# Two attention layers on one core: each engine keeps the order of emission in place of list scheduling

## The chip, the cores and the metric

The kernel runs on one core of a Trainium2 chip. The metric is the device time of one launch in microseconds; lower is better. Before the change it was 3159.26 us, the median of 3 runs (3157.74 to 3161.56).

A core has engines that run side by side, each through its own queue of instructions: TensorE (PE, with PEld for its weight loads), VectorE (DVE), ScalarE (ACT), GpSimd (POOL) and SyncE (SP, which here only issues DMAs). An engine waits for another through semaphores. The order of instructions inside each engine's queue is fixed when the program is built, and that order is what the change touches.

## What is computed

The input has 4 images of 64 x 64 tokens with 256 channels. Two layers of self-attention follow each other, cut here to their core:

```python
# layer 0: 32 query/key channels, 256 value channels
q = x @ Wq + bq; k = x @ Wk + bk; v = x @ Wv + bv
x = gamma * (softmax(q @ k.T) @ v) + x
# layer 1: 32 query/key channels, 128 value channels, output projection
f = x @ Wf + bf; g = x @ Wg + bg; v = x @ Wh + bh
x = x + (softmax(g @ f.T) @ v) @ Wo + bo
```

Each image attends over its own 4096 tokens; the softmax is taken without subtracting a maximum, and a general path (launched only if a flag says that the values are too large) stands behind the fast one.

## The kernel before

`fast_path` walks through 4 images, 2 layers each. A layer is cut into blocks of queries `j` (16 blocks of 256 queries in layer 0, 8 blocks of 512 in layer 1) and a block into steps `i` over the keys (8 steps of 512 keys in layer 0, 16 steps of 256 keys in layer 1). Every step handles a 128 x 1024 tile of scores:

- PE writes the scores `st` (line 532) into PSUM.
- ACT takes the exponential into `p` (544) and, where the step is "split", a slightly scaled one, rounded to the faster matmul format, into `high` (542). All steps of layer 0 and 6 of the 16 of a block in layer 1 are split.
- DVE makes from them `low` (555) and then `d` (560), the parts that restore the lost digits. In layer 1 DVE also adds `p` up (`p_sum`, 571 and 573); for 5 of the 16 steps DMAs issued by POOL add it into `p_sum_moved` instead (548, 550).
- PE multiplies the parts with the values: in layer 0 three products for each of two halves of the queries, 24 matmuls in all (582); in layer 1 either six matmuls of the parts or two of the whole `p` (600).

Some buffers are scarce: one tile `d` in layer 0, two tiles (tag `t`) that `high`, and in split steps of layer 1 `p` too, share, one `st` in PSUM (every other step of layer 1 uses the tile `pair`, which holds accumulators in layer 0), one set of accumulators (`acc0`, `acc1`, `pair`), two side tiles in PSUM, and one `p_sum_moved`.

At the end of a block ("turn" below) ACT and DVE copy the accumulators out: lines 615 and 616 in layer 0, 651 and 657 in layer 1, where 659 and 660 also close the sum of `p`. Then come small units of work that the plan spreads over the steps of the next block: in layer 0 the division and the residual (625, 626, 628, and an addition on POOL, 639); in layer 1 four outputs `pso` (667 and 668 on PE, 670 on DVE, 673 on ACT).

The next layer is prepared in units for 256 tokens, three pieces each: the transpose piece (392 on DVE, 405 `xh` on ACT, 406 `xl` on DVE), the query/key piece (422 on PE, 439 ACT, 440 DVE, 441 ACT, 442 DVE, then DMAs), and the value piece (464 on PE, 480 and 481 on ACT, and for split tiles 482 and 483 on DVE). The plan puts one unit into each block `j >= 2` of layer 0 (steps 0, 4 and 5) and about two into each block of layer 1 in the first three images. The first 6 units stand before the first step of all, 10 more in its first block.

The order in which the kernel emits all this is written out by hand. For each step it is

```python
s.cut_both()                 # DVE: d of this step
after.cut_low()              # DVE: low of the next step
s.add_up(p_sum)              # DVE, layer 1
if l == 1:
    if s.last: o = take_first_two(b, j, acc)      # ACT 651
    later.scores()           # PE 532, ACT 542 and 544, two steps ahead
    run(todo)                # the units of this step
    ...                      # PE: h, l or the whole p; d of the step before
else:
    ...                      # PE: h (and l)
    later.scores()
    run(todo)
    ...                      # PE: d (and l)
if s.last: ends = end_first(b, j, acc) if l == 0 else end_second(b, j, acc, p_sum, o)
```

In the kernel before, this order is only the input of the compiler's list scheduler, which places the instructions of each engine by its own estimate of when their operands are ready. In the profiled program it put, for instance, the copy `o` of a finished accumulator (615) ahead of two exponentials that were emitted earlier.

Of the kernel before, what the change touches and what calls it, by code (L numbers as in the profile page):

```python
# [824 lines left out]
def tile_two_attention_layers(tc: tile.TileContext, *args):  # L825
    nc = tc.nc
    with tc.tile_pool(name="flag", bufs=1) as pool:
        off = pool.tile([1, 1], I32, name="off")
        fast_path(tc, *args, off)
        flag = nc.values_load(off[0:1, 0:1], min_val=0, max_val=4 * P, skip_runtime_bounds_check_because="a count")  # L830
        with tc.If(flag > 0):
            general_path(tc, *args)
# [40 lines left out]
```

## Time and profile before

| | |
|---|---|
| median of the runs | 3159.26 us (3157.74 to 3161.56) |
| profiled execution: span, first to last instruction | 3154.1 us |
| median less span (what lies around the instructions; the profiled execution has no separate time) | 5.2 us |
| PE busy | 3116.3 us, 99% |
| DVE busy | 2689.1 us, 85% |
| ACT busy | 2140.1 us, 68% |
| POOL busy | 900.7 us, 29% |
| granted TensorE clock | 0.998 of full |

The profile shows one execution. Busy time is the time in which an engine had an instruction running; a line of the groups gives the number of instructions, the mean duration in ns, and the idle time just before them with what ended it. The timeline gives the start in us, the duration, the engine, the source line, the operation and its tiles; `x4` means four in a row. The windows view gives the busy time of each engine in a stretch.

### The profile page before, as it was taken

How to read it: one execution, taken by the hardware profiler on the slowest of the kernel's cores; microseconds unless marked ns; L12 is line 12 of the kernel's file. 1: busy time of each engine (PE TensorE's matmuls, PEld its weight loads, DVE VectorE, ACT ScalarE, POOL GpSimd, SP SyncE). 2: the span in 40 equal slices, each digit the busy share in tenths (PEclk: the TensorE clock that was granted, in tenths of full speed). 3: DMA queues.
4: the chain of work that ended last, by engine and by line, in shares of the span. 5: the costliest groups of instructions: out<-in, count | busy, mean ns of one | idle time of the engine just before them, and what ended most of it. 6: DMA issues, size and time to landing. Idle time of an engine off the chain costs nothing.

```text
span 3154.1 us, 54090 instructions
## 1 busy us (share of the span) xinstructions
PE 3116.3 (99%) x19908; PEld 2672.0 (85%) x19908; DVE 2689.1 (85%) x3237; ACT 2140.1 (68%) x2835; POOL 900.7 (29%) x1108
## 2 busy tenths in 40 slices
PE   8999999999999999999999999999999999999997
PEld 7999998666799999866679999976668999996664
DVE  7888888888888888888888888898888888888876
ACT  7666666777666666777766666677776666666674
POOL 5232224222422222422242222232223222233221
PEclk9999999999999999999999999999999999999999
DMA  4121114555512121555541112255554111125454
GB/s 119 43 53 47 48 48 104 107 108 105 104 44 51 41 53 47 113 101 112 107 93 47 49 45 51 51 116 107 105 113 81 48 46 47 49 65 105 97 95 73
DMA packets 391392, 239.49 MB, mean 76 GB/s; under 512 B 266672, under 2 KB 355248, under 8 KB 391120
## 3 DMA queue, kind: packets, MB, share of 16 engines
q0 software_dynamic: 68160, 134.86, 22.0%
q1 hardware_dynamic: 322048, 100.76, 13.4%
q8 instruction: 161, 2.64, 0.4%
q14 instruction: 111, 0.91, 0.1%
q10 hardware_dynamic: 912, 0.33, 0.1%
HBM read 82.58 MB, written 67.11 MB: 47 GB/s over the span
## 4 chain that ended last, share of the span: by engine, by line
PE 91%; DVE 3%; DMA 2%; issue 2%; ACT 1%; POOL 0%; SPq 0%; DVEq 0%; ACTq 0%; POOLq 0%
PE acc L600 24%; PE acc L582 23%; PE acc_pair L582 23%; PE st L532 14%; PE psv L464 4%; PE psqk L422 2%; PE pso L667 2%; DVE d L560 1%; DVE low L555 1%; ACT p L544 1%; DVE p_sum L573 1%; DMA p_sum_moved<-p 0%; DMA squares<-in_x 0%; PE pso L668 0%; DMA squares<-x_dram 0%
## 5 line engine op out<-in xcount | busy, mean ns | idle before, releaser
L542 ACT ACTIVATE high<-st,down 128x1024 fp32r<-128x1024 f32 x704 | 786.5, 1117 | 703.2 <-PE st L532 362.8
L544 ACT ACTIVATE p<-st 128x1024 f32<-128x1024 f32 x1024 | 1042.5, 1021 | 166.3 <-PE st L532 143.8
L560 DVE SCALAR_TENSOR_TENSOR d<-low,high 128x1024 fp32r<-128x1024 f32 x704 | 871.0, 1237 | 227.0 <-PE acc_pair L582 223.7
L555 DVE TENSOR_TENSOR low<-p,high 128x1024 fp32r<-128x1024 f32 x704 | 936.6, 1330 | 142.6 <-ACT p L544 141.6
L532 PE MATMUL st<-q,k 128*128 128x256 f32 (+1 forms) x3072 | 706.3, 338 | 2.5 <-DMA k<-qk_parts 1.4
L600 PE MATMUL acc<-p,v 128*128 128x512 f32 x1280 | 611.0, 597 | 0.0
L532 PEld LDWEIGHTS st<-q,k 128*128 128x128 f32 x3072 | 470.0, 189 | 103.3 <-issue 40.6
L639 POOL TENSOR_TENSOR x_res<-x,bo 128x256 f32<-128x256 f32 x128 | 212.5, 1660 | 879.3 <-DVE x L628 879.2
L600 PEld LDWEIGHTS acc<-p,v 128*128 128x128 f32 x1280 | 233.1, 189 | 161.8 <-issue 143.4
L573 DVE TENSOR_TENSOR p_sum<-p_sum,p 128x1024 f32<-128x1024 f32 x288 | 352.6, 1224 | 9.4 <-ACT p L544 5.8
L582 PE MATMUL acc<-v0h,high 128*128 128x258 f32 x2048 | 341.6, 284 | 1.2 <-ACT high L542 1.2
L582 PE MATMUL acc<-v0d,d 128*128 128x258 f32 x2048 | 339.2, 287 | 2.6 <-DVE d L560 2.2
L582 PE MATMUL acc<-v0l,low 128*128 128x256 f32 (+1 forms) x2048 | 329.3, 283 | 0.6 <-DVE low L555 0.5
L582 PE MATMUL acc_pair<-v0h,high 128*128 128x258 f32 x2048 | 329.8, 283 | 0.0
L582 PE MATMUL acc_pair<-v0l,low 128*128 128x256 f32 (+1 forms) x2048 | 328.8, 282 | 0.0
L582 PE MATMUL acc_pair<-v0d,d 128*128 128x258 f32 x2048 | 328.5, 282 | 0.0
L582 PEld LDWEIGHTS acc<-v0h,high 128*128 128x128 f32 x2048 | 286.0, 189 | 3.1 <-issue 1.4
L582 PEld LDWEIGHTS acc<-v0d,d 128*128 128x128 f32 x2048 | 281.5, 190 | 5.6 <-DVE d L560 4.9
L582 PEld LDWEIGHTS acc<-v0l,low 128*128 128x128 f32 x2048 | 282.2, 190 | 1.8 <-DVE low L555 1.3
L582 PEld LDWEIGHTS acc_pair<-v0h,high 128*128 128x128 f32 x2048 | 282.1, 189 | 0.0
L582 PEld LDWEIGHTS acc_pair<-v0l,low 128*128 128x128 f32 x2048 | 281.1, 189 | 0.0
L582 PEld LDWEIGHTS acc_pair<-v0d,d 128*128 128x128 f32 x2048 | 281.0, 189 | 0.0
(108 smaller groups left out, 3332.5 us busy)
## 6 DMA issues: line engine op xcount, KB each, us to landing
p_sum_moved<-p POOLq DMA_DIRECT2D x160, 512.0 KB, 4.7
x_res<-in_x SPq DMA_DIRECT2D x128, 128.0 KB, 2.1
qk_dram<-qk_parts SPq DMA_DIRECT2D x128, 128.0 KB, 1.9
x_dram<-x SPq DMA_DIRECT2D x128, 128.0 KB, 1.7
out<-x_res SPq DMA_DIRECT2D x128, 128.0 KB, 1.7
squares<-x_dram SPq DMA_DIRECT2D x512, 32.0 KB, 1.9
out<-y POOLq DMA_DIRECT2D x128, 128.0 KB, 3.2
q<-qk_dram POOLq DMA_DIRECT2D x252, 64.0 KB, 2.2
```

The lines of the kernel that those rows point to most:

```text
L422: nc.tensor.matmul(ps, wqk[l][:, c, :], x_parts[key][n][:, c, :], start=(c == n == 0), stop=(c == NCC - 1 and n == 1),)
L464: nc.tensor.matmul(ps[:, t, :], xT[key][:, c, t * P : (t + 1) * P], wv[l][:, c, :], start=(c == 0), stop=(c == NCC - 1),)
L532: nc.tensor.matmul(st[:, g, :], k_t[b, l, kt // NT][:, kt % NT * P : (kt % NT + 1) * P], q_t[b, l, j * n // QB][:, q0 : q0 + n], start=Tru ...
L542: nc.scalar.activation(self.high, s_flat, AF.Exp, bias=down)
L544: nc.scalar.activation(self.p, s_flat, AF.Exp)
L555: nc.vector.tensor_sub(self.low, self.p, self.high.bitcast(F32))
L560: nc.vector.scalar_tensor_tensor(self.d, self.low.bitcast(F32), -UP, self.high.bitcast(F32), ALU.mult, ALU.add)
L573: nc.vector.tensor_add(p_sum, p_sum, self.p)
L582: nc.tensor.matmul(acc[2 * s + which][:, :width], p[:, g * QB0 + s * P : g * QB0 + (s + 1) * P], v0[self.i][v][:, g, :width], start=self.f ...
L600: nc.tensor.matmul(acc[which], v_part[:, g, :], p[:, g * QB : (g + 1) * QB], start=first and g == 0, stop=last and g == G[1] - 1,)
L639: nc.gpsimd.tensor_add(x_old[s], x_new[s], bo_sb)
L667: nc.tensor.matmul(ps[:, :C], part, wo_sb, start=True, stop=True)
```

## The change

One `with` block is put around the call of `fast_path`. Inside it the list scheduler does not reorder: each engine's queue holds its instructions, and SP and POOL their DMA issues, in the order of emission. Tiles, instructions, buffers and dependencies stay as they are.

```diff
     with tc.tile_pool(name="flag", bufs=1) as pool:
         off = pool.tile([1, 1], I32, name="off")
-        fast_path(tc, *args, off)
+        with tc.manual_schedule():
+            fast_path(tc, *args, off)
         flag = nc.values_load(off[0:1, 0:1], min_val=0, max_val=4 * P, skip_runtime_bounds_check_because="a count")
```

The built programs differ as follows, engine by engine. PE has 20701 instructions in both, and 16677 of them stand at the same place. In layer 0 PE's order differs mainly around the turns, where the scheduler had pulled matmuls of the next step ahead. ACT and DVE differ around the turns and around every unit. SP and POOL change by a few places.

## The prediction

> **What bounds the kernel now.** I read the busy times and the chain that ended last, then the windows by layer, then the timeline of a turn in each layer.
>
> ```profile
> PE 3116.3 (99%) x19908; PEld 2672.0 (85%) x19908; DVE 2689.1 (85%) x3237; ACT 2140.1 (68%) x2835; POOL 900.7 (29%) x1108
> ...
> PE 91%; DVE 3%; DMA 2%; issue 2%; ACT 1%; POOL 0%; SPq 0%; DVEq 0%; ACTq 0%; POOLq 0%
> ```
>
> PE is never short of work: 38 us of its 3154 are idle, 16 of them in the first 100 us by the windows view. So a better order has little to win, while every wait that a new order puts in front of PE counts in full.
>
> ```profile
> 100.00:520.00 420.00, 419.81 (x3499) 418.85 (x3499) 364.76 (x426) 276.66 (x352) 118.33 (x120) 1.00 0.21 52
> 524.00:857.00 333.00, 332.22 (x1286) 224.31 (x1285) 291.45 (x353) 240.54 (x335) 94.69 (x138) 1.00 0.58 110
> 2851.00:3133.00 282.00, 281.74 (x989) 180.00 (x989) 227.79 (x244) 193.19 (x228) 73.80 (x97) 1.00 0.51 98
> ```
>
> These are layer 0 of an image, layer 1 with units of the next image in it, and layer 1 of the last image without them (columns: PE, PEld, DVE, ACT, POOL busy, clock, DMA). In the first two DVE is busy 87% (364.76 of 420, 291.45 of 333): it has little time to stand in a queue.
>
> The turn of layer 0 from block 5 to 6, as scheduled:
>
> ```profile
> 264.60 1.02 ACT L544 ACTIVATE p<-st 128x1024 f32<-128x1024 f32 x1
> 265.51 0.62 ACT L405 CAST xh<-xT 128x512 fp32r<-128x512 f32 x1
> 265.65 1.23 DVE L555 TENSOR_TENSOR low<-p,high 128x1024 fp32r<-128x1024 f32 x1
> 265.74 0.68 PE L532 MATMUL st<-q,k 128*128 128x256 f32 x4
> 266.01 0.40 ACT L615 ACTIVATE o<-acc 128x258 f32<-128x258 f32 x1
> ...
> 266.50 1.12 ACT L542 ACTIVATE high<-st,down 128x1024 fp32r<-128x1024 f32 x1
> ...
> 267.51 1.02 ACT L544 ACTIVATE p<-st 128x1024 f32<-128x1024 f32 x1
> 267.70 0.64 PE L582 MATMUL acc<-v0h,high 128*128 128x258 f32 x4
> 267.94 1.22 DVE L560 SCALAR_TENSOR_TENSOR d<-low,high 128x1024 fp32r<-128x1024 f32 x1
> ```
>
> Two things to see: ACT copies the accumulator at 266.01, before the two exponentials, so that PE can overwrite it at 267.70 without a gap; and `xh` (transpose piece) sits in a hole of ACT. Four matmuls of this kind follow the next four at 0.48 us (267.70 to 268.18), so a plain step of 28 costs 3.35 us.
>
> **The change, part by part.** It removes and adds no work. I walk through the emitted order with the durations of these rows and ask when PE must wait. Between engines I take 0.05 to 0.1 us, and from the start of scores to the exponential 0.76 (265.74 to 266.50).
>
> *Turn of layer 0.* In emission order ACT does `high` and `p` first: 266.5 + 1.12 + 1.02 gives 268.63; `o` ends at 269.03. PE, ready at 267.58, waits 1.5 us for the accumulator. DVE adds the two `o` (0.42 each, to 269.95) before `d` (to 271.2), which PE needs at 271.0: 0.2 more. PE ends the step at 272.7; before, the same matmuls were done at 270.94. **1.75 us, 64 turns: 112.**
>
> *Transpose piece (step 0).* DVE transposes (0.70), then waits for `xh`, which stands behind the two exponentials of the step: `xh` ends at 274.1, `xl` 274.8, the queued `d` 276.05. PE wants it at 275.07. **1.0 us, 14 blocks per image, 56: 56.**
>
> *Query/key piece (step 4).* The chain copy 0.37, add 0.47, cast 0.41, subtract 0.42 goes four times between ACT and DVE, begins behind `p`, and now stands whole before `d` on DVE: `d` is ready about 0.75 us after PE asks, even with the value matmuls (0.95 us) as cover. **56 x 0.75: 42.** *Value piece (step 5):* for the 6 of 14 tiles that are split, two DVE operations wait for ACT and delay `d` by 1.65 us. **24 x 1.65: 40.** The other 8 cost nothing: the cover is 1.5 us of slack on ACT; gone, they would cost up to 0.8 each.
>
> *POOL beside DVE.* After a residual, POOL's addition slows `low`:
>
> ```profile
> 246.66 1.80 POOL L639 TENSOR_TENSOR x_res<-x,bo 128x256 f32<-128x256 f32 x1 [1.56 <-DVE x L628]
> ...
> 247.78 1.76 DVE L555 TENSOR_TENSOR low<-p,high 128x1024 fp32r<-128x1024 f32 x1
> ```
>
> 1.76 against 1.23 us: 0.53, twice per block, hidden today by about 0.9 us of slack; the walk leaves 0.2. I take 0.3 per block, **20** (0 to 64). [...] The row shows 0.53, and the sum goes by the row.
>
> Layer 0: **270** (low end 112, the turns alone; high 340).
>
> *Layer 1.* Its turn from block 2 to 3 in the trace:
>
> ```profile
> 642.64 1.22 DVE L659 TENSOR_TENSOR p_sum<-p_sum,p_sum_moved 128x1024 f32<-128x1024 f32 x1
> ...
> 644.44 0.55 POOL L548 DMA_DIRECT2D p_sum_moved<-p  x1 [6.92 <-ACT qk L439]
> ...
> 644.91 0.68 DVE L660 TENSOR_TENSOR sums<-p_sum 128x512 f32<-128x512 f32 x1
> ...
> 645.74 0.30 PE L668 MATMUL pso<-ones,sums 128*128 128x1 f32 x2
> ...
> 648.28 1.02 ACT L544 ACTIVATE p<-st 128x1024 f32<-128x1024 f32 x1 [0.51 <-DMA p_sum_moved<-p]
> ```
>
> Here the scheduler let PE run the queries/keys and a whole step before 668, and ACT an exponential of a later step before the one at 648.28 (which needs the buffer that the DMA of 644.44 reads, 3.84 us). In emission order both stand in line. Counting from the scores of step 1 of the new block: DVE does `low` (1.49), `p_sum` (2.7), transpose and, after `xh`, `xl` (4.8), the two `o` (5.7), 659 (6.9), 660 (7.6); PE's first `pso` then starts at 7.6 in place of 4.5: 3.1 us. The DMA starts after 659, so `p` of step 3 ends at 11.9, and behind it in ACT's queue stand `y`, which frees a side tile, and the query/key copy; PE waits for both before `pso` 1 and the value matmuls, then for `high` of step 5, which waits for `d` of step 3. At step 7 of this block PE is 6 us late, and two further units cost 2.8 at steps 11 to 15 (`p` of step 13 waits for `p_sum`, that waited for `xl` and the value piece). Block 3: 8.9 us. The same walk of block 5, with units at other steps: 7.5. Mean **8.2, 24 blocks: 197.** Without units `pso` waits 1.0 and smaller waits 0.5: **1.5 x 8: 12.** Layer 1: **209** (low 90 if half of the waits overlap; high 300).
>
> *Start.* Six units run before the first scores, which come at about 38 us in place of 22.3; the interleaved rest was slow before as well, so I take **10** (0 to 25).
>
> Sum 270 + 209 + 10 = 489: 3154.1 + 489 + 5.2 = **3648; I say 3650.**
>
> SP and POOL: 8 loads `squares` take 0.5 us each to issue and follow the query/key piece, whose store is now up to 2 us later; the next transpose comes 4 or 5 steps later (13 us), so nothing.
>
> *The clock.* The granted clock is 1.00 in all three windows, and the waits PE does have there are under 1 us. [...] The gaps of the walk stay at 1 to 3 us, and the sum has nothing for them.
>
> **The rivals.**
>
> *The waits overlap (0.17).* An engine freed by one stall of PE catches up, so that only the turns count: 112 + 24 x 3.1 + 8 x 1.0 + 10 = 204, thus 3363. For it: DVE has 13% spare. Against it: in the walk the waits lie 2 or more steps apart, and PE's delay does not shorten DVE's queue.
>
> *Faster (0.04).* The scheduler breaks groups: in the built program 21 of the 320 groups of whole-`p` matmuls in layer 1 are broken in two. After such a group the next takes 0.4 us more than otherwise (619.09 to 619.95 against 0.46), so 21 x 0.4 = 8 us come back, and PE's 38 idle us could shrink by a third: 3139. It decides only if all the queues' waits stay below PE's slack of about 0.9 us per step; at the turn of layer 0 `o` alone stands 2.1 us later.
>
> *It does nothing (0.02).* 16677 of PE's 20701 places are the same; if ACT's and DVE's order did not matter, 3159 within 6 us. DVE's order differs at every unit, which speaks against it.
>
> *Worse than walked (0.07).* DVE, 87% busy, becomes the bound in layer 1 with every wait on ACT in its queue, and PE's gaps grow beyond 3 us: 12 us per block, 24 x 3.8 = 91 more, and layer 0 at its high end, 70: 3810.
>
> **The numbers.** Forecast 3650 at 0.70. Its own low end is 112 + 90 + 0 = 202 (the first rival's place), its high end 340 + 300 + 25 = 665, 3824. Ends do not fall together, so I take 3420 to 3820, which leaves out most of the first rival and the small cases. About 0.2% (6 us) is what a measurement can tell from no change: faster 0.04, same 0.02, slower 0.94.
>
> **What would show it.** Right: PE's busy share falls to 84 to 88%; the period of a layer 0 block grows from 28.2 us to about 31.7, and to 33.3 where the value tile is split; a block of layer 1 grows by 7 to 10 us in the first three images and by 1 to 2 in the last; idle before 582 is put down to `o` of line 615 and to `d`, and before 668 to `sums`. Wrong: blocks of layer 0 at 30 us (only the turn counts), or PE idle that is put down to DMAs, or a clock below 1.00.

## The result, and the profile after

The changed kernel takes 3642.19 us (median of 4 runs, 3639.95 to 3644.05) against 3158.95 us for the kernel before (4 runs, 3157.74 to 3161.56): the ratio is 1.1534, with a 95% interval of 1.152 to 1.1548. The profiled execution took 3644.05 us with a span of 3642.3 us, 488.2 us more than the span before.

First the busy times and the chain that ended last:

```profile
PE 3274.0 (90%) x19908; PEld 2723.9 (75%) x19908; DVE 2722.6 (75%) x3237; ACT 2149.1 (59%) x2835; POOL 868.7 (24%) x1108
...
PE 46%; DVE 20%; ACT 19%; issue 8%; DMA 5%; POOL 1%; ACTq 0%; SPq 0%; DVEq 0%; POOLq 0%
```

No engine has more instructions than before, and none is full any more. PE holds 46% of the chain that ended last, DVE and ACT together 39%. Before, 91% of it lay on PE.

The windows of layer 0, of layer 1 with pieces of the next image, and of layer 1 of the last image (PE, PEld, DVE, ACT, POOL busy, then the clock and the DMA share):

```profile
140.00:580.00 440.00, 403.98 (x3266) 394.25 (x3265) 342.63 (x394) 258.73 (x329) 96.31 (x92) 1.00 0.17 43
612.00:945.00 333.00, 298.10 (x1046) 189.30 (x1046) 248.56 (x299) 206.06 (x287) 68.32 (x95) 0.97 0.48 92
3345.00:3610.00 265.00, 254.30 (x870) 158.45 (x868) 202.26 (x212) 172.54 (x197) 68.24 (x95) 0.99 0.49 92
```

PE is idle 36 us of 440, 35 of 333 and 11 of 265, and in layer 1 the clock is no longer 1.00.

The waits of PE by what ended them (us in total, times, longest):

```profile
PE acc L582 <- DVE d L560: 100.7, 136, 2.3
PE acc L582 <- ACT o L615: 59.6, 60, 1.0
PE pso L668 <- DVE sums L660: 35.1, 29, 1.5
PE st L532 <- DMA q<-qk_dram: 30.2, 14, 4.7
...
PE psqk L422 <- ACT y L673: 17.0, 8, 3.5
...
PE st L532 <- DMA k<-qk_dram: 11.2, 4, 3.0
```

The first three and the wait for `y` are ones that the prediction named. The two DMA waits it had not.

The turn of layer 0 from block 5 to 6, with the transpose piece behind it:

```profile
287.88 1.12 ACT L542 ACTIVATE high<-st,down 128x1024 fp32r<-128x1024 f32 x1 [1.14 <-PE st L532]
...
288.89 1.02 ACT L544 ACTIVATE p<-st 128x1024 f32<-128x1024 f32 x1
289.80 0.39 ACT L615 ACTIVATE o<-acc 128x258 f32<-128x258 f32 x1
...
290.24 0.75 PE L582 MATMUL acc<-v0h,high 128*128 128x258 f32 x4 [1.00 <-ACT o L615]
290.56 0.42 DVE L616 TENSOR_TENSOR o<-o,acc_pair 128x258 f32<-128x258 f32 x1
...
290.89 1.22 DVE L560 SCALAR_TENSOR_TENSOR d<-low,high 128x1024 fp32r<-128x1024 f32 x1
...
293.53 1.01 ACT L544 ACTIVATE p<-st 128x1024 f32<-128x1024 f32 x1
...
294.43 0.62 ACT L405 CAST xh<-xT 128x512 fp32r<-128x512 f32 x1
...
295.08 0.69 DVE L406 TENSOR_TENSOR xl<-xT,xh 128x512 fp32r<-128x512 f32 x1 [1.22 <-ACT xh L405]
...
295.69 1.22 DVE L560 SCALAR_TENSOR_TENSOR d<-low,high 128x1024 fp32r<-128x1024 f32 x1
...
296.96 0.75 PE L582 MATMUL acc<-v0d,d 128*128 128x258 f32 x4 [0.72 <-DVE d L560]
```

The copy `o` now stands directly behind `high` and `p`, and PE waits 1.00 us for it. In the next step `xh` stands behind `p` on ACT, so `xl` waits 1.22 us at the head of DVE's queue with `d` behind it, and PE waits 0.72 us for that `d`.

The turn of layer 1 from block 2 to 3 in the first image, the one that the prediction walks through:

```profile
758.90 0.70 PE L667 MATMUL pso<-wo,o 128*128 128x256 f32 x2 [0.97 <-DVE o L657]
759.09 1.22 DVE L659 TENSOR_TENSOR p_sum<-p_sum,p_sum_moved 128x1024 f32<-128x1024 f32 x1
760.35 0.69 DVE L660 TENSOR_TENSOR sums<-p_sum 128x512 f32<-128x512 f32 x1
760.89 0.56 POOL L548 DMA_DIRECT2D p_sum_moved<-p  x1 [17.19 <-DVE p_sum L659]
760.96 1.22 DVE L560 SCALAR_TENSOR_TENSOR d<-low,high 128x1024 fp32r<-128x1024 f32 x1
...
761.09 0.38 PE L668 MATMUL pso<-ones,sums 128*128 128x1 f32 x2 [1.49 <-DVE sums L660]
...
762.29 1.11 ACT L542 ACTIVATE high<-st,down 128x1024 fp32r<-128x1024 f32 x1 [3.58 <-DVE inverse L670]
...
763.84 1.03 ACT L544 ACTIVATE p<-st 128x1024 f32<-128x1024 f32 x1 [0.44 <-DMA p_sum_moved<-p]
...
765.29 0.70 PE L667 MATMUL pso<-wo,o 128*128 128x256 f32 x2 [0.59 <-ACT y L673]
```

PE waits 0.97 us for `o` and 1.49 us for the sums and, at the next output, 0.59 us for `y`. In between ACT stands still for 3.58 us, until DVE is through with the closing of the old block and with `d` (760.96) of the new one. (The profile names 670, the short operation of DVE that follows that `d`.)

### The profile page after: what moved, and what is told of

It reads as the page before. It is cut to its first block, busy times and chain, and to the rows that moved or that the text cites. A ratio compares the mean times of both kernels' runs of the same rounds, so it can differ in the third digit from the quotient of the medians.

```text
span 3642.3 us, 53692 instructions
## 1 busy us (share of the span) xinstructions
PE 3274.0 (90%) x19908; PEld 2723.9 (75%) x19908; DVE 2722.6 (75%) x3237; ACT 2149.1 (59%) x2835; POOL 868.7 (24%) x1108
## 4 chain that ended last, share of the span: by engine, by line
PE 46%; DVE 20%; ACT 19%; issue 8%; DMA 5%; POOL 1%; ACTq 0%; SPq 0%; DVEq 0%; POOLq 0%
PE acc L582 15%; PE acc_pair L582 12%; ACT p L544 8%; PE st L532 7%; PE acc L600 7%; DVE d L560 7%; ACT high L542 6%; DVE low L555 3%; PE psv L464 2%; DMA p_sum_moved<-p 2%; DVE p_sum L573 2%; DVE xl L406 2%; ACT xh L405 2%; DVE qk L440 1%; DMA q<-qk_dram 1%
## 5 line engine op out<-in xcount | busy, mean ns | idle before, releaser
L532 PE MATMUL st<-q,k 128*128 128x256 f32 (+1 forms) x3072 | 710.0, 340 | 67.4 <-DMA q<-qk_dram 30.2
L600 PE MATMUL acc<-p,v 128*128 128x512 f32 x1280 | 625.6, 612 | 0.0
L582 PE MATMUL acc<-v0d,d 128*128 128x258 f32 x2048 | 355.5, 296 | 100.8 <-DVE d L560 100.7
L582 PE MATMUL acc<-v0h,high 128*128 128x258 f32 x2048 | 341.5, 289 | 59.6 <-ACT o L615 59.6
L639 POOL TENSOR_TENSOR x_res<-x,bo 128x256 f32<-128x256 f32 x128 | 200.3, 1565 | 759.5 <-DVE x L628 759.1
L751 POOL TENSOR_TENSOR x_res<-x_res,bv 128x256 f32<-128x256 f32 x128 | 152.4, 1210 | 708.3 <-DMA x_res<-in_x 605.8
```

What stands on the lines that cost most here:

```text
L532: nc.tensor.matmul(st[:, g, :], k_t[b, l, kt // NT][:, kt % NT * P : (kt % NT + 1) * P], q_t[b, l, j * n // QB][:, q0 : q0 + n], start=Tru ...
L582: nc.tensor.matmul(acc[2 * s + which][:, :width], p[:, g * QB0 + s * P : g * QB0 + (s + 1) * P], v0[self.i][v][:, g, :width], start=self.f ...
L600: nc.tensor.matmul(acc[which], v_part[:, g, :], p[:, g * QB : (g + 1) * QB], start=first and g == 0, stop=last and g == G[1] - 1,)
L639: nc.gpsimd.tensor_add(x_old[s], x_new[s], bo_sb)
L751: nc.gpsimd.tensor_add(x_res[b, j][t], x_res[b, j][t], bv)
```

## The experiments

The times are those of one run each, for e_final the median of 4; each is compared with the kernel before, run beside it on the same chip (3158.55 to 3162.98 us). What a run gains or loses against the changed kernel is counted from 3642.19. Runs of one kernel lie up to 6.4 us apart (e_final), so a difference of that size between single runs says nothing. The table gives, from the traces, the mean time from one block to the next (from the scores of step 2 to those of the next block, in layer 1 seven such intervals per image; "split" are the blocks of layer 0 with a value piece that is split), the change from layer 0 to layer 1 (the same from the last block of layer 0), and the time at half clock (a granted clock of 0.50 in the records) up to the last matmuls, in us.

| kernel | time | layer 0, plain | layer 0, split | change of layer | layer 1, images 0-2 | layer 1, image 3 | half clock |
|---|---|---|---|---|---|---|---|
| before | 3159 | 28.2 | 28.4 | 28.9 | 40.0 | 35.4 | 0 |
| changed | 3642 | 31.4 | 32.8 | 37.9 | 47.5 | 38.0 | 140 |
| m_l0 | 3415 | 31.4 | 32.8 | 36.8 | 40.1 | 35.5 | 41 |
| m_l1 | 3379 | 28.3 | 28.5 | 29.6 | 47.7 | 38.9 | 89 |
| m_pe | 3291 | 29.3 | 29.3 | 29.7 | 42.0 | 36.4 | 34 |
| m_act_dve | 3519 | 30.6 | 32.3 | 32.8 | 46.8 | 36.7 | 48 |
| e_turn1 | 3610 | 30.9 | 32.3 | 37.6 | 47.6 | 37.9 | 123 |
| e_turn2 | 3622 | 31.2 | 32.6 | 38.2 | 47.6 | 38.0 | 126 |
| e_turn3 | 3574 | 30.1 | 31.6 | 36.6 | 47.6 | 40.6 | 140 |
| e_units0 | 3505 | 29.9 | 29.8 | 30.2 | 47.5 | 38.3 | 102 |
| e_units1 | 3656 | 31.4 | 32.8 | 38.1 | 48.6 | 39.3 | 164 |
| e_pso | 3649 | 31.4 | 32.8 | 37.7 | 48.3 | 38.2 | 123 |
| e_act1 | 3626 | 31.5 | 31.5 | 36.1 | 47.9 | 40.5 | 116 |
| e_final | 3438 | 29.0 | 28.9 | 29.8 | 47.1 | 40.1 | 109 |

### Which layer: m_l0 and m_l1

The order of emission is kept only in the steps of one layer; m_l1 has `l == 1`.

```diff
+    region = ExitStack()
     for n, s in enumerate(steps):
         b, l, j = s.b, s.l, s.j
+        if s.first and j == 0:
+            region.close()
+            if l == 0:
+                region.enter_context(tc.manual_schedule())
...
+    region.close()
```

Expected of m_l0:

> Order of emission in layer 0 of each image alone (and in the units of layer 1 that its blocks carry); layer 1 and the six units ahead of the first step list-scheduled as before. Theory (waits are local to a layer and add up): blocks of layer 0 at 31.4 and 32.8 us as in the changed kernel, blocks of layer 1 at 40.4 us as before; 3159 + about 193 (plain blocks) + 42 (last blocks) + a part of the start's 36 gives 3390 to 3430. Rival (the layers spoil each other, for instance through a clock that stays low behind a stretch of gaps): layer 0 alone brings less than 150, thus under 3310, with blocks below 30 us.

Expected of m_l1:

> Order of emission in layer 1 of each image alone; layer 0 list-scheduled as before. Theory: blocks of layer 1 at 48 to 49 us in the first three images and 37 in the last, blocks of layer 0 at 28.2; 3159 + about 166 + 12 + 17 + a part of the 20 of the change of layer gives 3350 to 3375, and the two halves of the change add up to its 483 within 40. The clock is then below 1.00 in layer 1 alone. Rival (coupling): under 3300, and layer 0 and layer 1 alone together make less than 350 of the 483.

Measured: 3415.01 and 3378.53 us against 3160.49 us before, so 254.5 and 218.0; together 472.5 of the 481.7 that the changed kernel (3642.19) lies above the same run. The layers' losses are their own and add up, as the theory had it; the rival falls. In m_l1 layer 0 is back at 28.3 us, in m_l0 layer 1 at 40.1. m_l1 came out 4 us above its range.

### Which engine: m_pe and m_act_dve

Here the region stands around the whole of `fast_path` again, but for some engines alone.

```diff
-        with tc.manual_schedule():
+        with tc.manual_schedule(engines={mybir.EngineType.PE}):
```

Expected of m_pe:

> Order of emission on PE alone; ACT, DVE, POOL and SP list-scheduled. Theory (what makes PE late is the order on ACT and DVE, in front of it): PE waits at the turns of layer 1 only, where it now asks for the sums a step early, some 1 to 3 us in 24 blocks; 3159 + 25 to 75, thus 3180 to 3235, with blocks of layer 0 below 28.6 us. Rival (PE's own order, with its matmuls no longer pulled ahead at the turns and units, carries the loss): over 3400.

Expected of m_act_dve, with `Activation` and `DVE` in the set:

> Order of emission on ACT and DVE alone; PE, POOL and SP list-scheduled. Theory: nearly the whole loss stays, since PE can't pull ahead what needs d and o; 3560 to 3650. Rival (an order of PE that is chosen for the waits can fill them with other matmuls): under 3400.

Measured: 3290.97 and 3518.73 us against 3160.49, so 130.5 and 358.2. Together that is 488.7, near the whole of 481.7, though stage by stage the two do not add up so well: 2.0 and 6.8 of 7.5 us in a block of layer 1, 0.8 and 3.9 of 9.0 at the change of layer. (POOL and SP are scheduled in both; their order was not tried alone.) Both values lie between theory and rival. ACT and DVE carry three quarters; PE's own order costs more than expected, and in layer 0 too. The waits of PE in m_pe show where:

```profile
PE acc_pair L582 <- DVE o L616: 47.8, 60, 1.1
```

60 of the 64 turns, 0.8 us each: DVE adds the second `o` when the scheduler thought it due, and PE, which now keeps to its order, asks earlier. With PE free to reorder (m_act_dve) the wait for `o` of 615 is no longer among its larger ones, and one for the exponential takes its place:

```profile
PE st L532 <- ACT p L544: 82.6, 145, 2.1
PE acc L582 <- DVE d L560: 69.0, 142, 1.3
```

### The turn of layer 0: e_turn1, e_turn2 and e_turn3

e_turn1 emits the copy of the first accumulator ahead of the scores and exponentials of the last step:

```diff
+            if s.last:
+                o = [copy_first(b, j, acc, 0)]
             later.scores()
```

> The changed kernel, but in the last step of a layer 0 block the copy of the first accumulator (line 615, first half) is emitted ahead of the scores and exponentials of a later step. Theory (two waits stand one behind the other at the turn: o, then d of the next step, which stands behind both additions of o on DVE): PE's wait for o of line 615 (60 us) goes, but the one for d grows from 100 to about 150; 0.5 us come back per turn, 32 of 3642, thus 3600 to 3620. Rival (o alone is the turn's loss): all 1.75 us of 64 turns, 3530.

Measured: 3609.81 us, 32 less than the changed kernel; layer 0 gains 0.5 us per block. The theory holds in size. The wait that comes next is not all where it was expected, though: PE's wait for `d` did not grow, and PE waits for the second `o` instead (line 616 has moved to 619):

```profile
PE acc L582 <- DVE d L560: 90.7, 136, 2.3
...
PE acc_pair L582 <- DVE o L619: 30.2, 60, 0.5
```

e_turn2 also puts the addition to the second `o` of the block before (kept in `late`) behind `d`:

```diff
         s.cut_both()
+        run(late)
+        late.clear()
         after.cut_low()
```

> As the run before it, and the addition to the second o (line 616) is emitted behind d of the next step. Theory: both waits of the turn go; 64 x 1.3 to 1.75, thus 83 to 112 less than the changed kernel: 3530 to 3560, and blocks of layer 0 at 29.8 and 31.3 us. Rival (PE then waits for the second addition, which frees the accumulator in pair, for as long as before for d): no better than the run before it, over 3590.

Measured: 3622.47 us, 13 more than e_turn1, with blocks of layer 0 at 31.2 and 32.6 us in place of 30.9 and 32.3. The rival was right: `d` still waits as long, and the second addition is now waited for half as long again.

```profile
PE acc L582 <- DVE d L560: 99.9, 135, 2.2
PE acc_pair L582 <- DVE o L619: 45.5, 60, 1.0
```

So not the additions are in the wrong place but the second copy, which still stands behind the exponentials on ACT. e_turn3 moves both copies, and the products that they wait for, ahead:

```diff
-            for half in () if edge else (0, 1):
+            for half in (1,) if s.last else () if edge else (0, 1):
                 s.products_first(acc, half, "l")
...
+            if s.last:
+                o = [copy_first(b, j, acc, half) for half in range(NS)]
             later.scores()
             run(todo)
-            for half, what in ((0, "d"), (1, "l"), (1, "d")) if edge else ((0, "d"), (1, "d")):
+            for half, what in ((0, "d"), (1, "l"), (1, "d")) if s.first else ((0, "d"), (1, "d")):
```

> The changed kernel, but in the last step of a layer 0 block the products of the second half with low are emitted ahead of the scores, and then both copies of line 615, ahead of the scores and their exponentials. Theory (the turn's whole loss comes from the two copies standing behind two exponentials, and the additions and d behind the copies): 64 x 1.75 = 112 less, blocks of layer 0 at 29.7 and 31.1 us, no wait for o of 615 or 616 left: 3525 to 3545. Rival (d of the next block's first step is late by itself, behind low, and takes over): less than 50, over 3590.

Measured: 3574.18 us, 68 less, between the two. Layer 0 gains 1.3 and 1.2 us per block. That is all that the turn had cost (1.27 us, shown below) and three quarters of the 1.75 that the theory took for it. No wait for `o` is left among PE's larger waits. 18 us of the gain were lost again in layer 1 of the last image (40.6 in place of 38.0 us, 7 blocks), whose order the edit does not touch. There PE's waits for the load of `q` came to 13.2 us in place of 4.3.

### The pieces: e_units0, e_units1, e_act1

e_units0 leaves the turn and emits DVE's half of each piece one step later, behind `d` and `low` of that step (`put_off` keeps an operation for the next step, `run(due)` emits it; the query/key piece spreads over three steps):

```diff
             nc.scalar.copy(x_parts[key][0], xT[key])
-            nc.vector.tensor_sub(x_parts[key][1], xT[key], x_parts[key][0].bitcast(F32))
+            put_off(lambda: nc.vector.tensor_sub(x_parts[key][1], xT[key], x_parts[key][0].bitcast(F32)))
...
         s.add_up(p_sum)
+        due, off_dve[:] = off_dve[:], []
+        run(due)
```

> The changed kernel, but what DVE does for the transpose, query/key and value pieces in blocks of layer 0 (406, 440, 442, 482, 483; and with them 441 and the stores) is emitted one step later, behind d and low of that step. The turn is left as changed. Theory (these operations wait for ACT in DVE's queue, with d behind them): of the 3.2 and 4.6 us by which blocks of layer 0 grew only the turn's 1.75 stays; 32 x 1.45 + 24 x 2.85 = 115 less: 3510 to 3550, blocks alike at 29.9 to 30.2 whether the value tile is split or not. Rival (DVE has no room in the step after either, and low of the next step becomes late in place of d): less than 50, over 3590.

Measured: 3505.28 us, 137 less, 5 us below the theory's range. Blocks of layer 0 take 29.9 us whether split or not, the time that the theory gave (though not from the turn alone, see below), and the wait for `d` is all but gone while the one for `o` stays (596 and 629 are 582 and 615 before, 574 is 560):

```profile
PE acc L596 <- ACT o L629: 59.6, 60, 1.0
...
PE acc L596 <- DVE d L574: 8.7, 9, 2.2
```

The rest of the gain, 4 x 7.7 us, is the change of layer, which fell from 37.9 to 30.2. The edit changes POOL's order there too: the last keys of the next layer, whose store comes later, are now loaded behind `q`:

```profile
1431.87 1.98 POOL L507 DMA_DIRECT2D q<-qk_dram  x4
...
1443.43 1.97 POOL L507 DMA_DIRECT2D k<-qk_dram  x4
```

e_units1 does the same in blocks of layer 1 alone.

> The changed kernel, but what DVE does for the three pieces in blocks of layer 1 is emitted one step later, as was done for layer 0. Theory (the walk: xl, the value piece and the query/key copies in DVE's queue make high and p of later steps late through d and p_sum; 2.8 us per block at the late units, and some of the turn's 3.1 since xl stands ahead of the sums): 24 x 3 to 5, thus 70 to 120 less: 3520 to 3570, blocks of layer 1 in the first three images at 44 to 46 us. Rival (in layer 1 the waits of the turn, sums, y and the moved sums, are the loss, the pieces lie beside them): less than 30, over 3610.

Measured: 3656.42 us, 14 more. The theory falls; the rival's numbers hold, but new waits came in, so the run does not show that the pieces lay beside the loss. The query/key piece stands only 2 steps of 2.5 us behind the transpose piece in layer 1, so now PE waits for `xl` and `xh`, 61 us in all:

```profile
PE psqk L429 <- DVE xl L413: 32.5, 40, 1.8
PE psqk L429 <- ACT xh L412: 28.3, 11, 4.0
```

e_act1 moves the other half: ACT's operations of a piece go ahead of the two exponentials of the step, in both layers.

```diff
             later.scores()
-            run(todo)
+            run(u for u in todo if "end_second" not in u.__qualname__)
+            later.exponentials()
+            run(u for u in todo if "end_second" in u.__qualname__)
```

> The changed kernel, but of each step the exponentials (542, 544) are emitted behind the pieces of that step, in both layers; the scores on PE, the four outputs of layer 1 and the copies of the turn stay where they are. PE's and DVE's orders are those of the changed kernel, so this moves ACT's operations alone (405, 439, 441, 480, 481 ahead of two exponentials in place of behind them). Theory (DVE's waits for ACT, 139 us for xh, 153 for the copy of the queries and keys, 91 for the value piece, come from this order, in layer 1 too, and deferring DVE's half was the wrong end to move there): layer 0 gains its 80 to 115, layer 1 50 to 120: 3410 to 3510, and blocks of layer 1 at 44 to 46 us. Rival (ACT now waits for DVE inside the pieces, and its exponentials become late): over 3580.

(In layer 1 a few places on PE and DVE change as well, where an output and a piece share a step: in the traces 192 of PE's 19908 instructions and 108 of DVE's 3237 stand elsewhere.) Measured: 3625.81 us, 16 less; the rival holds. Split and plain blocks of layer 0 are now equal, but at 31.5 us. ACT, in order, now waits for DVE inside the pieces, its exponentials are late, and PE waits for them. The waits of ACT, then those of PE:

```profile
ACT xh L405 <- DVE xT L392: 356.7, 112, 5.3
```

```profile
PE st L532 <- ACT p L548: 133.0, 165, 2.7
```

A piece goes back and forth between two queues that are in order. In these runs one of the two queues waited at its head where its operations stood close together: DVE up to 5.3 us for `xh` in the changed kernel, ACT up to 5.3 us for `xT` in e_act1. In layer 0 distance (e_units0) took the wait out, and PE's for `d` fell from 100.7 us to 8.7; in layer 1 (e_units1) one step was not distance enough, and PE waited 61 us for `xl` and `xh`.

### The outputs of layer 1: e_pso

```diff
             for n, u in enumerate(ends):
-                put(1 + n, u)
+                put(2 + n, u)
```

> The changed kernel, but in layer 1 the four outputs of the block before are emitted one step later (steps 2 to 5 in place of 1 to 4). Theory (PE asks for sums before DVE has them): the waits for sums and o (35 + 6 us) go and some of the half-rate windows of the clock with them; 40 to 70 less, 3570 to 3600. Rival (the wait is handed on to y, which frees the side tile for the query/key piece, and to the exponentials behind it): less than 20, over 3620.

Measured: 3649.1 us, 7 more, hardly above the scatter of the runs, but no gain: the rival. The wait for the sums is gone from PE's larger waits, and others have its place:

```profile
PE psqk L422 <- ACT y L673: 26.1, 9, 4.3
...
PE acc L600 <- DVE d L560: 19.9, 27, 1.0
PE pso L667 <- ACT y L673: 15.0, 14, 1.6
```

### All that helped, together: e_final

> The changed kernel with three edits of the emitted order: the turn's copies ahead of the exponentials as in e_turn3; DVE's half of the pieces one step later in layer 0 as in e_units0; and in layer 1 the same for the pieces of the next image alone, with query/key and value piece 3 and 5 steps behind the transpose piece in place of 2 and 3 (in e_units1 PE waited 61 us for xl and xh since the query/key piece followed too soon). Theory (turn and pieces add up, and in layer 1 the pieces are the part that was left): blocks of layer 0 at 28.5 to 28.8 us, 137 + 68 less; blocks of layer 1 in the first three images at 44 to 46.5, 45 to 95 less: 3345 to 3395. Rival A (behind the turn another wait stands in layer 0): blocks of layer 0 over 29.3. Rival B (in layer 1 the turn's outputs and the clock are the loss, whatever the pieces do): blocks of layer 1 at 48 or more, and 3420 or more in all.

The edits are those of e_turn3 and e_units0, with `put_off` for the pieces of the next image in layer 1 as well, and:

```diff
-                for n, u in zip((0, 2, 3), project_units(b + 1, 0, h)):
+                for n, u in zip((0, 3, 5), project_units(b + 1, 0, h)):
```

Measured: 3438.27 us (4 runs, 3434.89 to 3441.31) against 3158.55; ratio 1.0881, 95% interval 1.0863 to 1.0899. Layer 0 is at 29.0 and 28.9 us, 0.2 above the theory and below rival A: its two causes add up, and 2.4 of 3.2 us (3.9 of 4.4 in split blocks) are undone by the place of a few operations. Layer 1 stays at 47.1: by its total (3438, over 3420) rival B holds, though by its blocks it is just under the bound of 48. No order of emission that was tried comes near the list scheduler's.

## Why the prediction was right, and where it was not

The forecast was 3650 us and the time is 3642. The growth of 488 us sits, stage by stage, as follows. (Layer 0: 60 intervals between blocks, 228.0 us, less 13 in the first block of all, which is counted as start, and with a usual 3.2 us for each of the 4 last blocks, 13. Start: 19.1 us up to the first block's step 2 and those 13. Change of layer: 35.8 less 13. Layer 1 is the rest.)

| | predicted | measured |
|---|---|---|
| layer 0, blocks | 270 | 228 |
| layer 1, blocks and turns | 209 | 205 |
| start | 10 | 32 |
| change from layer 0 to 1 | 0 | 23 |

The total came out within 8 us partly by luck: layer 0 was forecast 42 us too high, the start and the change of layer together 45 us too low. Two of the prediction's own signs of being wrong, PE idle that is put down to DMAs and a clock below 1.00, did appear.

**Right.** The mechanism: in the changed kernel queues in order hand each other's waits to PE, which waits 100.7 us for `d`, 59.6 for `o` and 35.1 for the sums (before, 38 us for everything). The blocks, 31.4 us against "about 31.7" and 32.8 against 33.3. Layer 1 without pieces, 1 to 2 us: the blocks of the last image took 37.0 to 37.5 us where 35.5 stood before (its first and last interval, at 41.9 and 38.2, apart). The rival in which the waits overlap until only the turns count fell: e_units0 alone gave back 137 us.

**Layer 0, term by term.** Within a block, the times from the scores of one step to those of the next show where it grew. (Means of the blocks from 2 on. The scores of step 2 come in step 0, and so on; the turn is the sum of the three intervals around it, since the scheduler had moved its scores. The value piece is taken in the split blocks, the other rows in the plain ones. The rows that the prediction shows for its turn of layer 0 are those from block 6 to 7, counted from 0; the turns are alike.)

| us per block | walked | before | changed | growth |
|---|---|---|---|---|
| turn | 1.75 | 10.11 | 11.38 | 1.27 |
| transpose piece (scores of step 3 to 4) | 1.0 | 3.35 | 4.35 | 1.00 |
| query/key piece (7 to 0) | 0.75 | 4.25 | 5.03 | 0.78 |
| value piece, split (0 to 1) | 1.65 | 2.87 | 4.36 | 1.49 |
| POOL beside DVE (5 to 6) | 0.3 | 3.34 | 3.47 | at most 0.13 |

So the pieces cost what the walk gave them, and the turn was mis-sized. PE waits 1.00 us for `o` where the walk had 1.5, and in the rows shown no wait for `d` follows in the first step, where it had 0.2. The walk added the full durations of `high` and `p`, 2.14 us; in the rows above they and `o` start 1.01 and 0.91 us apart. The time from block 1 to 2, with no piece in it, agrees: 28.14 us, and 26.90 in e_turn3, which repairs the turn.

POOL beside DVE cost nothing by itself: between blocks 1 and 2, where POOL's additions run but no piece does, no interval but the turn's grew. With a piece close by something is left, 0.13 us here and 0.43 in e_units0 (scores of steps 4 to 6), where the put-off `xl` comes just ahead of the additions:

```profile
1153.82 1.76 DVE L569 TENSOR_TENSOR low<-p,high 128x1024 fp32r<-128x1024 f32 x1
...
1157.64 0.54 PEld L596 LDWEIGHTS acc<-v0d,d 128*128 128x128 f32 x4 [0.26 <-DVE d L574]
```

So e_units0's blocks stand 1.7 us above before by a turn of 1.27 and these 0.43; its theory hit the 1.7 with a turn of 1.75 alone, which was luck. In the prediction's rows for POOL 0.68 us of the addition's 1.80 are left when `low` starts (246.66 + 1.80 less 247.78), and `low` takes 0.53 us longer than its usual 1.23.

**Missed: the queues that were costed at nothing.** The prediction said of SP and POOL "so nothing". At the change of layer, POOL's queue before and after:

```profile
1289.55 1.99 POOL L493 DMA_DIRECT2D q<-qk_dram  x4 [4.42 <-PE st L532]
1292.56 1.95 POOL L493 DMA_DIRECT2D k<-qk_dram  x4 [1.02 <-issue]
```

```profile
1501.95 1.94 POOL L493 DMA_DIRECT2D k<-qk_dram  x4 [5.45 <-DMA squares<-x_dram]
1503.87 1.94 POOL L493 DMA_DIRECT2D q<-qk_dram  x4
...
1508.35 1.19 PE L532 MATMUL st<-q,k 128*128 128x512 f32 x2 [4.28 <-DMA q<-qk_dram]
```

The scheduler had put the load of `q` ahead of the last keys, which are wanted many steps later. In emission order it stands behind them, starts when they were able to start, and PE waits 4.28 us. PE's idle time put down to DMAs is 30.2 us for `q`, 17.7 of it at the four changes of layer, and 11.2 for `k`, of 368 us idle. Where `q` goes ahead of the last keys the wait is missing: in e_units0 (30.2 us per change) and in m_act_dve, whose POOL is scheduled (32.8). How much the place is worth by itself is not shown, since both runs differ in other queues too, and in m_l0 the change takes 36.8 us though PE waits there for `xh` (4.1 to 4.4 us) and not for `q`. The miss did not overturn the forecast, but the step was wrong: a few places in a queue can matter when they concern what is wanted next.

**Missed: the clock.** The sum had nothing for it, on gaps of 1 to 3 us in the walk. The runs bear that out for the short ones alone: in the changed kernel the clock stayed at 1.00 in the window of layer 0, where PE's waits for `d` and `o` reach 1.2 us, and it fell to 0.50 behind a single wait of 1.76 us (718.15, last section). Up to the last matmuls the records show 140 us at a granted clock of 0.50 (the kernel before: none). PE was busy for 129 us of that. If work takes at most twice as long at 0.50, an estimate from the granted clock, it cost at most half of them, 65 us, and less where PE would have waited anyway. (Four matmuls of line 582 took 1.06 us at 1509.34, at half clock, in place of 0.64, and the next four followed at 0.85 in place of 0.48.) PE's busy share, 90% in place of 84 to 88, is in part this slowness: the same four matmuls count as busy for longer.

**Layer 1: right in sum and in the block that was walked, not settled in its parts.** In the turn shown the sums are ready 7.3 us after the scores of step 1 of the new block (753.73), where the walk has 7.6; PE waits 0.97 + 1.49 = 2.46 us at the first output, where it has 3.1; `p` ends at 11.1 in place of 11.9; and PE is 5.4 us late at step 7 in place of 6. Block 3 grew by 9.2, 8.7 and 9.2 us in the three images (walked: 8.9), block 5 by 9.6, 9.6 and 8.0 (7.5). But the blocks differ more than these two show, from 4.0 to 12.3 us, with a mean of 7.7 against 8.2.

PE's idle time in 21 blocks of the first three images is 100.4 us of a growth of 156 (before, 2): 30 us for the sums and `o` (660, 657), 26 for `y`, 16 for `low` of a split step and 14 for `p`, the rest smaller. Of the other 56 us, the half clock (51 us, PE busy for 48.5 of them) makes at most 24 by the same estimate; the remainder was not traced. (The two matmuls of line 668 took 0.38 us at 761.09, behind their wait, and 0.30 in the prediction's row.) What the runs show is that the loss is layer 1's own (m_l1) and that most of it comes from the order on ACT and DVE (46.8 of 47.5 us with PE scheduled). Four edits, of the outputs, of DVE's and of ACT's half of the pieces and of the pieces' distance, left it between 47.1 and 48.6. The closing of the sums (657 to 660), which stands ahead of `d` of the new block on DVE and for which ACT waits 3.58 us in the rows shown, was not moved. Which part carries the loss stays open.

**Start, 32 in place of 10.** In m_l0, where the units ahead of the first step are scheduled, the first scores of step 2 come at 45.4 us, with 57.2 in the changed kernel and 38.1 before. So about 12 us are the six units; the other 20 fall behind them, up to the end of the first block, with the ten units that the prediction took for slow already. Up to there 31 us ran at half clock (PE busy for 28 of them, so at most 14 us of the loss by that estimate); before, the records show none.

## What to carry to other kernels

With queues in order, the price of a place was here not the operation's own time but what stands behind it (the two copies `o` take 0.4 us each, and the turn grew by 1.27 us). Put copies that free a buffer ahead of long work for later steps, and put the halves of a chain that goes back and forth between two engines further apart than the other engine's long work (one step of 3.35 us was enough in layer 0, one of 2.5 us in layer 1 was not). When an order changes, walk every queue, the DMA issuers' too, and ask of each place that moved who wants its result next. Moving one wait handed most or all of it to the next resource in e_turn2 (13 us more than e_turn1), e_pso (7 more than the changed kernel) and e_act1 (16 less, where 130 to 230 were expected), so a repair is to be measured with the waits of all engines, not of one.

## What was not expected of the hardware

The granted clock fell to 0.50 behind a single wait of 1.76 us. The windows view at a turn of layer 1 in the changed kernel (columns as above; the last three are the granted clock, the DMA share and GB/s):

```profile
715.41:718.82 3.41, 1.65 (x11) 1.43 (x10) 3.41 (x5) 0.51 (x2) 1.31 (x2) 1.00 0.85 136
718.82:725.65 6.83, 6.00 (x16) 4.35 (x15) 3.30 (x6) 4.52 (x7) 1.29 (x2) 0.50 0.57 88
725.65:729.06 3.41, 3.41 (x13) 2.17 (x13) 1.24 (x2) 1.32 (x4) 0.86 (x1) 1.00 0.72 97
```

```profile
718.15 0.39 PE L422 MATMUL psqk<-xh,wqk 128*128 128x256 f32 x1 [1.76 <-ACT y L673]
```

In the first stretch PE is busy for 1.65 of 3.41 us, all of its idle time being the one wait of 1.76 us, and the clock is at half for the next 6.83. In the 13 traces of this case with more than one change of clock (the kernel before has one, at its end) the changes stand on a grid of 3.41 us, in the changed kernel within 0.03 us, and the busy share of PE in one such window mostly tells what follows. Of windows at full clock in all 14 traces in which PE was busy less than 40%, 193 of 193 were followed by half clock; between 40 and 60%, 139 of 339; above 60%, 6 of 13308. In the changed kernel alone it is 22 of 22, 12 of 24 and 0 of 968. The wait of 1.76 us in the rows above is half of one window, and such a window did not always bring the clock down, as the middle group shows. The counts say how often it fell in these traces, not why.
